# An expert's rank from the sign of a score difference, in two fused operations, in a one-core transformer block

## The chip, the core and the metric

The kernel runs on one core of a Trainium2 chip. The metric is the device time of one execution in microseconds (us). The engines are named as in the profile: PE (TensorE, matrix products), PEld (its weight loads), DVE (VectorE), ACT (ScalarE), POOL (GpSimd) and SP (SyncE, which here mostly issues DMAs). Every engine takes its own instructions strictly in the order in which the program emits them; between engines, semaphores hold an instruction back until its data or its buffer is there.

## The reference

A block of two attention layers, each followed by a mixture-of-experts feed-forward layer, on 2048 tokens of 256 numbers. What matters here is how each token's two experts are chosen:

```
scores = jax.nn.sigmoid(x @ router_w.T)              # [tokens, 8 experts]
selection_scores = scores + expert_bias
_, top_idx = jax.lax.top_k(selection_scores, TOPK)   # TOPK = 2
top_scores = jnp.take_along_axis(scores, top_idx, axis=-1)
top_scores = top_scores / (top_scores.sum(-1, keepdims=True) + 1e-09)
```

`top_k` puts the lower index first where two scores are equal. Everything is float32. The feed-forward layer runs twice (kernel layers 1 and 3), with the same weights.

## The kernel before, in words

The tokens are cut into four blocks (`tb`) of 512. The program is emitted by one long loop of *steps* (from line 1255 on). A step emits, in this order: matrix products of attention scores for two pairs of heads (L508); the reads of their results, by DVE for row maxima (L540, L552) and by ACT for exponentials (L603, L605); then, twice, a *half*, in which waiting small pieces are emitted; and at the end of the step the *fill*: pieces of the shared feed-forward (PE L921, L934 and L948; ACT L924; DVE L925, L937 and L950) and of the routed experts (PE L993, L1009 and L1030; DVE L995, L1017 and L1019).

The small pieces of DVE wait in the queue `vector`. Each stands there with a cost in us that the planner assumes for it. In each half the loop adds to an allowance and emits pieces while the allowance is above zero:

```
share = BUSY.get(i, VECTOR)                                  # VECTOR = 0.8
spare = min(spare + busy * share, 2 * busy * share)
while vector and spare > 0:
    us, f = vector.popleft()
    f()
    spare -= us
```

Here `i` counts the steps and `busy` is 1 while attention steps remain, 4 after that, so the allowance is capped at 1.6 in most steps. What is emitted for PE, ACT, POOL and SP comes from other queues (`queue`, `fill`, `routed_fill`, `moves`, `later`), whose budgets don't read the allowance.

Routing runs once for each block in each of the two feed-forward layers: eight times. `routing` (L718) emits the router's products and, at the end of that step, a tanh on ACT (L752). Then its DVE pieces follow, each appended to `vector` when the one before has been emitted (`chain`, L257): `selection` (L756, L757: the score and the biased score `sel`), `better` (L761), `equal` (L764), `equal_before` (L767), `ranks` (L770, L771), `best` (L774 to L776), `chosen` (no instruction), then `shares` (L780 to L783). The rank of an expert is the number of experts with a larger score, and of those with an equal score and a lower index; `other` and `own` are two views of `sel`, so each of these operations has 4 x 8 x 8 = 256 numbers in each of 128 partitions. `lower` is a constant table of ones and zeros, one where the other expert's index is lower.

Where a routing completes a group of tokens (seven of the eight times), `chosen` also starts `places` (L801): `either` (L822), a count on PE (L829) that is emitted in the step after `either`, and again DVE pieces (`along`, `tiling`, `starts`, `pick`, `rows_known`, `passed`, `weights`, `pick`, L844 to L882). They give the rows to which POOL scatters the tokens (L898) and the experts whose weights it fetches (L971). The pieces of a layer norm (L284 to L314) go through the same queue `vector`: `stats`, `guess` (L292 to L294), `newton` (L299 to L301) and `apply`.

In the order of time the eight routings are those of layer 1, blocks 0 to 3, and of layer 3, blocks 0 to 3. They are called routing 1 to 8 below. In routings 4 and 6 the loop emits a projection of the attention (PE L697, DVE L705) from `queue` in the same two halves.

Of the kernel before, what the change touches and what calls it, by code (L numbers as in the profile page):

```python
# [16 lines left out]
ALU = mybir.AluOpType  # L17
# [34 lines left out]
def tile_block(ctx: ExitStack, tc: tile.TileContext, a: dict, out: bass.AP):  # L52
    nc = tc.nc
# [93 lines left out]
    lower = const.tile([P, NX, NX], F32, tag="lower", name="lower")  # L147
# [67 lines left out]
    def free_one(at):  # L215
        n, j = at[:2]
        returned.add((n, j))
        if (n, 1 - j) in returned:
            returned.difference_update([(n, 0), (n, 1)])
            pairs.append(n)  # L220
# [16 lines left out]
    def alone(at, ins):  # L237
        n, j, user, other = at
        own = ins.ins.engine
        tc.add_to_no_dep_group(f"user{user}_{own}", ins.ins)  # L240
        for e in (mybir.EngineType.PE, mybir.EngineType.DVE, mybir.EngineType.Activation):
            if e != own and other is not None:
                tc.declare_no_dep(ins.ins, group=f"user{other}_{e}", reason="another bank of the pair")
# [13 lines left out]
    def chain(*steps):  # L257
        def add(i):
            if i < len(steps):
                q, f, *us = steps[i]  # L260
                f = partial(run, i, f)
                if us:
                    q.append((us[0], f))
                elif i:
                    after(0, partial(q.append, f))
                else:
                    q.append(f)

        def run(i, f):
            f()  # L270
            add(i + 1)

        add(0)
# [54 lines left out]
    def few_outputs(kind, xt, weights, to):  # L328
        bank, pr = one(kind)
        for c in range(EC):  # L330
            for t in range(TB // P):
                alone(bank, nc.tensor.matmul(
                    pr[t * FEW : (t + 1) * FEW, 0:P],
                    weights[:, c, :],
                    xt[:, c, t * P : (t + 1) * P],
                    start=(c == 0),
                    stop=(c == EC - 1),
                ))
        alone(bank, nc.scalar.copy(to, pr[:, 0:P]))
        free_one(bank)  # L340

    def tokens_down(kind, rows):
        bank, pt = one(kind)
        pt = pt[:, 0:P]
        alone(bank, nc.tensor.transpose(pt, rows, ident))
        return bank, pt.rearrange("p (t e) -> p t e", e=FEW)
# [364 lines left out]
    def sorting(ln, tb):  # L711
        return next(f for f, (l, tbs) in enumerate(SORTED) if l == ln and tb in tbs)
# [5 lines left out]
    def routing(ln, tb, then):  # L718
        xt = xts[ln, tb]
        nt = TB // P  # L720
        n = f"{ln}_{tb}"
        f = sorting(ln, tb)
        tbs = SORTED[f][1]
        t0 = tbs.index(tb) * nt
        if t0 == 0:
            picks[f] = (
                fp.tile([P, 2, len(tbs) * nt, NX], F32, tag="picked", name=f"picked{f}", bufs=1),
                fp.tile([P, len(tbs) * nt, NX], F32, tag="cw", name=f"cw{f}", bufs=1),
            )
        m0, m1 = (picks[f][0][:, k, t0 : t0 + nt, :] for k in range(2))  # L730
        cw = picks[f][1][:, t0 : t0 + nt, :]

        def small(x, shape):
            return fp.tile(shape, F32, tag=x, name=f"{x}{n}", bufs=1)

        sg, sel, rank, top = (small(x, [P, nt, NX]) for x in ("sg", "sel", "rank", "top"))
        tot = small("tot", [P, nt])
        full = [P, nt, NX, NX]
        gt, eq = small("gt", full), small("eq", full)
        other = sel.unsqueeze(2).broadcast_to(full)  # L740
        own = sel.unsqueeze(3).broadcast_to(full)

        rated = small("rated", [P, P])

        def scores():
            few_outputs("router", xt, late["router"], rated)
            chain(*after_scores)


        def rates():  # L750
            bank, pt = tokens_down("rated", rated)
            alone(bank, nc.scalar.activation(sg, pt[:, :, 0:NX], AF.Tanh, scale=0.5))  # L752
            free_one(bank)

        def selection():
            nc.vector.tensor_scalar(sg, sg, 0.5, 0.5, ALU.mult, ALU.add)  # L756
            nc.vector.tensor_tensor(sel, sg, late["ebias"].unsqueeze(1).broadcast_to([P, nt, NX]), ALU.add)  # L757


        def better():  # L760
            nc.vector.tensor_tensor(gt, other, own, ALU.is_gt)  # L761

        def equal():
            nc.vector.tensor_tensor(eq, other, own, ALU.is_equal)  # L764

        def equal_before():
            nc.vector.tensor_tensor(eq, eq, lower.unsqueeze(1).broadcast_to(full), ALU.mult)  # L767

        def ranks():
            nc.vector.tensor_tensor(gt, gt, eq, ALU.add)  # L770
            nc.vector.tensor_reduce(rank, gt, AX.X, ALU.add)  # L771

        def best():
            nc.vector.tensor_scalar(m0, rank, 0.5, None, ALU.is_lt)  # L774
            nc.vector.tensor_scalar(m1, rank, 1.0, None, ALU.is_equal)
            nc.vector.scalar_tensor_tensor(top, rank, 1.5, sg, ALU.is_lt, ALU.mult)  # L776


        def shares():
            nc.vector.tensor_reduce(tot, top, AX.X, ALU.add)  # L780
            nc.vector.tensor_scalar(tot, tot, 1e-9, None, ALU.add)
            nc.vector.reciprocal(tot, tot)
            nc.vector.scalar_tensor_tensor(  # L783
                cw, top, 0.5, tot.unsqueeze(2).broadcast_to([P, nt, NX]), ALU.mult, ALU.mult
            )

        def chosen():
            then()
            vector.append((0.7, shares))

        v = [(selection, 0.35), (better, 0.45), (equal, 0.45), (equal_before, 0.45), (ranks, 0.9), (best, 0.55)]
        queue.append(scores)
        after_scores = ((closing, rates), *[(vector, x, us) for x, us in v], (vector, chosen, 0.0))

# [325 lines left out]
    def ffn(ln, tb):  # L1120
        f = sorting(ln, tb)
        last = tb == SORTED[f][1][-1]
        routing(ln, tb, partial(places, f) if last else lambda: None)
        h0, y0 = shared_pieces(ln, tb, 0)
        h1, y1 = shared_pieces(ln, tb, 4)
        y1.append((0.0, partial(shared_end, ln, tb)))
        fill.extend(h0 + h1[:2] + y0 + h1[2:] + y1)
        if last:
            sorting_now.add(f)
# [293 lines left out]
```

## Time and profile before

| what | value |
|---|---|
| time of three runs | median 1227.33 us, from 1226.06 to 1230.43 |
| the profiled execution's own time | 1226.37 us |
| its span, from first to last instruction | 1224.7 us |
| mean granted TensorE clock | 0.978 |
| instructions in all | 21600 |
| ACT busy | 473.8 us (39%) |
| POOL busy | 385.2 us (31%) |
| first operation of the rank (L761) in routings 1, 2, 3, 4 | at 176.00, 317.63, 471.54 and 598.27 us |
| and in routings 5, 6, 7, 8 | at 747.08, 895.14, 974.32 and 1129.35 us |

The durations come from one profiled execution. A row of the groups reads: line, engine, operation, result and source, shapes, count, then busy us and mean ns of one, then the idle time of the engine before such instructions with what ended it. A row of the timeline reads: start, duration, engine, line, operation, and in brackets the idle time before it and who ended that. An instruction's duration is longer than the distance to the start of the next one where the two overlap, so a saving is read from the distances of starts, not from durations.

### The profile page before, as it was taken

What the parts mean: (1) busy time and instruction counts of PE and PEld (TensorE: products, weight loads), DVE (VectorE), ACT (ScalarE), POOL (GpSimd) and SP (SyncE); (2) the same over time, 40 slices, a digit from 0 to 9 for tenths busy, and PEclk for the clock granted to TensorE, in tenths of its full rate; (3) what the DMA queues carried; (4) which work ended last, traced back from release to release, by engine and by line L of the source; (5) the groups of instructions that cost most, each with busy time, mean ns of one, the idle gap of its engine ahead of it and who ended that gap; (6) DMA issues with size and microseconds to landing.
All of it is one profiled execution on the core that took longest, in us unless ns stands there. A gap on an engine that the chain in (4) does not pass through costs nothing.

```text
span 1224.7 us, 21600 instructions
## 1 busy us (share of the span) xinstructions
PE 1151.4 (94%) x7684; PEld 661.8 (54%) x7684; DVE 803.8 (66%) x2308; ACT 473.8 (39%) x838; POOL 385.2 (31%) x568
## 2 busy tenths in 40 slices
PE   5889999999999999998999999999999999998985
PEld 2343444465655556465654656456654553666563
DVE  5677878658776868646776867565678675335444
ACT  1356544435443542443234444444313445331110
POOL 3131201523252311543242212345311135142643
PEclk8789999999999999999999999999999999998998
DMA  7131010313442433434541423245422113464763
GB/s 232 42 123 33 11 43 25 126 50 114 147 148 70 133 111 97 135 105 123 172 151 56 139 78 99 78 134 173 126 70 70 56 43 111 149 202 139 250 231 108
DMA packets 87500, 137.85 MB, mean 113 GB/s; under 512 B 24016, under 2 KB 58704, under 8 KB 87264
## 3 DMA queue, kind: packets, MB, share of 16 engines
q1 hardware_dynamic: 68064, 66.63, 17.8%
q0 software_dynamic: 17520, 68.74, 17.5%
q8 instruction: 61, 1.00, 0.3%
q10 hardware_dynamic: 1808, 1.10, 0.3%
q14 instruction: 47, 0.39, 0.1%
HBM read 93.80 MB, written 31.59 MB: 102 GB/s over the span
## 4 chain that ended last, share of the span: by engine, by line
PE 44%; issue 4%; DVE 4%; DMA 3%; ACT 1%; SPq 1%; POOL 1%; POOLq 0%; ACTq 0%; DVEq 0%
PE ps L508 10%; PE ps L921 6%; PE ps L948 6%; PE ps L934 5%; PE ps L634 5%; PE ps L1009 4%; PE ps L1030 2%; PE ps L396 2%; DMA xr<-sx 1%; PE ps L697 1%; PE ps L993 1%; DMA wt<-in_w_e_dram,wrow 1%; PE ps L357 1%; PE ps L468 1%; ACT e L603 1%
## 5 line engine op out<-in xcount | busy, mean ns | idle before, releaser
L540 DVE CUSTOM_DVE_ANT_0 junk<-ps,hidden 128x384 f32<-128x384 f32 (+3 forms) x512 | 250.4, 489 | 86.2 <-PE ps L508 60.1
L508 PE MATMUL ps<-k,q 32*128 32x512 f32 (+3 forms) x1536 | 286.3, 523 | 18.0 <-DVE nm L540 6.4
L508 PE MATMUL ps<-q,k 32*128 32x512 f32 (+3 forms) x1536 | 279.9, 517 | 3.9 <-DVE nm L540 2.2
L603 ACT ACTIVATE e<-ps 128x512 f32<-128x512 f32 (+1 forms) x320 | 160.1, 552 | 221.9 <-PE ps L508 211.4
L614 POOL TENSOR_SCALAR_AFFINE_SELECT e<-e 128x256 f32<-128x256 f32 x256 | 100.9, 409 | 369.0 <-ACT e L603 240.5
L508 PEld LDWEIGHTS ps<-k,q 32*128 32x128 f32 x1536 | 111.1, 189 | 129.3 <-issue 45.6
L552 DVE TENSOR_REDUCE mx<-ps 128x2 f32<-128x1024 f32 x128 | 150.7, 1217 | 26.0 <-PE ps L508 25.2
L605 ACT ACTIVATE e<-ps 128x1024 f32<-128x1024 f32 (+1 forms) x160 | 151.1, 944 | 23.1 <-PE ps L508 14.5
L634 PE MATMUL ps<-e,v 128*17 128x512 f32 (+3 forms) x1536 | 137.1, 493 | 5.7 <-POOL e L614 3.8
L971 POOL DMA_INDIRECT wt<-in_w_e_dram,wrow x98 | 94.4, 963 | 131.8 <-PE ps L1030 111.2
L508 PEld LDWEIGHTS ps<-q,k 32*128 32x128 f32 x1536 | 114.0, 184 | 38.4 <-issue 7.7
L921 PE MATMUL ps<-xt,w 128*128 128x512 f32 x256 | 124.5, 609 | 0.5
L934 PE MATMUL ps<-xt,w 128*128 128x512 f32 x256 | 123.3, 604 | 0.0
L948 PE MATMUL ps<-w,h 128*128 128x256 f32 x512 | 117.1, 382 | 0.0
L948 PEld LDWEIGHTS ps<-w,h 128*128 128x128 f32 x512 | 95.3, 190 | 22.6 <-ACT e L603 5.1
L1009 PE MATMUL ps<-xst,wt 128*128 128x128 f32 x784 | 98.1, 278 | 1.0 <-DMA wt<-in_w_e_dram,wrow 1.0
L1009 PEld LDWEIGHTS ps<-xst,wt 128*128 128x128 f32 x784 | 93.4, 194 | 2.0 <-DMA wt<-in_w_e_dram,wrow 1.5
L634 PEld LDWEIGHTS ps<-e,v 128*17 128x17 f32 x1536 | 41.9, 98 | 97.2 <-issue 60.7
L898 POOL DMA_INDIRECT sx<-xh,pos x64 | 62.5, 976 | 80.3 <-PE ps L634 25.8
L925 DVE SCALAR_TENSOR_TENSOR h<-h,ps 128x512 f32<-128x512 f32 x64 | 43.8, 685 | 63.7 <-ACT h L924 63.5
L1044 POOL DMA_INDIRECT yg<-sy,pos x64 | 62.3, 974 | 68.7 <-DVE x L1052 37.4
L934 PEld LDWEIGHTS ps<-xt,w 128*128 128x128 f32 x256 | 46.0, 190 | 57.7 <-issue 43.9
(142 smaller groups left out, 1166.8 us busy)
## 6 DMA issues: line engine op xcount, KB each, us to landing
w<-in_w_dram SPq DMA_DIRECT2D x64, 256.0 KB
xr<-sx SPq DMA_DIRECT2D x53, 256.0 KB
sy<-yt SPq DMA_DIRECT2D x53, 256.0 KB
sx<-hidden POOLq DMA_DIRECT2D x2, 2944.0 KB, 15.6
q<-stage SPq DMA_DIRECT2D x24, 224.0 KB
uc<-u SPq DMA_DIRECT2D x128, 32.0 KB
rb<-dr SPq DMA_DIRECT2D x128, 32.0 KB
den<-u SPq DMA_DIRECT2D x128, 2.0 KB
```

What stands on the lines that cost most here:

```text
L508: nc.tensor.matmul(pair[:, j, at : at + c1 - c0], lhs[r, l0 : l0 + P], rhs[r, c0:c1], start=True, stop=True)
L540: r = nc.vector.tensor_tensor_reduce(junk[:, 0:wd], pair[:, j, at : at + wd], hidden_keys[:, TB - wd : TB], -1.0, -NEG, ALU.add, ALU.min, ...
L552: nc.vector.tensor_reduce(mx[:, 2 * pr : 2 * pr + 2, ts[0]], pair, AX.X, ALU.max, negate=True)
L603: alone(at, nc.scalar.activation(e[:, 2 * pr + j, c0:TB], pair[:, j, c0:TB], AF.Exp))
L605: nc.scalar.activation(e[:, 2 * pr : 2 * pr + 2, c0:TB], pair[:, :, c0:TB], AF.Exp)
L614: nc.gpsimd.affine_select(out=blk, in_=blk, compare_op=ALU.is_ge, fill=0.0, base=0, pattern=[[0, 2], [1, P]], channel_multiplier=-1,)
L634: alone(bank, nc.tensor.matmul(av[g * 32 : g * 32 + D + 1, c0:TB], v[:, i, 0 if multi_query(w) else g4 * 4 + g, :], e[:, g, at : at + TB - ...
L921: mm = nc.tensor.matmul(pg, loaded[i][:, k, 0:P], xts[ln, tb][:, k, :], start=(k == 0), stop=(k == EC - 1))
L934: mm = nc.tensor.matmul(pl, w[:, k, P : 2 * P], xts[ln, tb][:, k, :], start=(k == 0), stop=(k == EC - 1))
L948: alone(bank, nc.tensor.matmul(po[:, k, :], hs[i0 + i][:, cols], late["w3"][:, c0 + i, :], start=(i == 0), stop=(i == 3)))
L971: nc.gpsimd.indirect_dma_start(w, None, a["w_e"], by_row(wrow[:, j : j + 1]))
L1009: mm = nc.tensor.matmul(gu[:, j, k, :], w[:, cols], xt[:, c, k, :], start=(c == 0), stop=(c == EC - 1))
```

## The change

The comparison and the test for equality no longer read the two views of `sel` each. One operation takes their difference; two fused operations compare it with zero, one multiplying by the table `lower`, the other adding the first one's result. The piece `equal` is gone from the list, with its planned 0.45 us; the other planned costs stand as they were.

```diff
-        def better():
-            nc.vector.tensor_tensor(gt, other, own, ALU.is_gt)
-
-        def equal():
-            nc.vector.tensor_tensor(eq, other, own, ALU.is_equal)
+        def ahead():
+            nc.vector.tensor_tensor(gt, other, own, ALU.subtract)
 
         def equal_before():
-            nc.vector.tensor_tensor(eq, eq, lower.unsqueeze(1).broadcast_to(full), ALU.mult)
+            nc.vector.scalar_tensor_tensor(
+                eq, gt, 0.0, lower.unsqueeze(1).broadcast_to(full), ALU.is_equal, ALU.mult
+            )
 
         def ranks():
-            nc.vector.tensor_tensor(gt, gt, eq, ALU.add)
+            nc.vector.scalar_tensor_tensor(gt, gt, 0.0, eq, ALU.is_gt, ALU.add)
             nc.vector.tensor_reduce(rank, gt, AX.X, ALU.add)
...
-        v = [(selection, 0.35), (better, 0.45), (equal, 0.45), (equal_before, 0.45), (ranks, 0.9), (best, 0.55)]
+        v = [(selection, 0.35), (ahead, 0.45), (equal_before, 0.45), (ranks, 0.9), (best, 0.55)]
```

## The prediction, made before the run

> **What bounds the kernel now.** I read the page's busy times and its chain that ended last, then PE's own waits.
>
> ```profile
> PE 1151.4 (94%) x7684; PEld 661.8 (54%) x7684; DVE 803.8 (66%) x2308; ACT 473.8 (39%) x838; POOL 385.2 (31%) x568
> ...
> PE 44%; issue 4%; DVE 4%; DMA 3%; ACT 1%; SPq 1%; POOL 1%; POOLq 0%; ACTq 0%; DVEq 0%
> ```
>
> PE is busy for 94% of the span, so 73 us of idle PE are all that a faster DVE could win anywhere. DVE has a third of its time free. The change touches DVE alone, eight times, so the question at each place is whether PE stands still there for DVE's sake. Of PE's waits, two belong to lines that follow a routing:
>
> ```profile
> PE ps L508 <- DVE nm L540: 8.6, 10, 2.7
> ...
> PE ps L508 <- DVE h L925: 1.7, 3, 0.8
> ```
>
> The columns are us in total, times, and the longest.
>
> **What an operation costs.** From the groups by shape:
>
> ```profile
> L1052 DVE SCALAR_TENSOR_TENSOR x<-yg,share,x 128x256 f32<-128x256 f32 x64 | 30.7, 483 | 6.7 <-DMA yg<-sy,pos 5.6
> ...
> L1017 DVE SCALAR_TENSOR_TENSOR ht<-ht,ps 128x256 f32<-128x256 f32 x53 | 22.2, 419 | 58.3 <-ACT ht L1014 58.3
> ...
> L767 DVE TENSOR_TENSOR eq<-eq,lower 128x256 f32<-128x256 f32 x8 | 3.4, 430 | 0.3
> L761 DVE TENSOR_TENSOR gt<-sel 128x256 f32<-128x256 f32 x8 | 3.4, 424 | 0.3
> L770 DVE TENSOR_TENSOR gt<-gt,eq 128x256 f32<-128x256 f32 x8 | 3.4, 423 | 0.2
> ...
> L764 DVE TENSOR_TENSOR eq<-sel 128x256 f32<-128x256 f32 x8 | 3.3, 418 | 0.0
> ```
>
> The removed operation (L764) lasts 418 ns, but the distance of starts is what counts. Routing 1 in the timeline:
>
> ```profile
> 176.00 0.42 DVE L761 TENSOR_TENSOR gt<-sel 128x256 f32<-128x256 f32 x1
> 176.34 0.42 DVE L764 TENSOR_TENSOR eq<-sel 128x256 f32<-128x256 f32 x1
> 176.79 0.42 DVE L767 TENSOR_TENSOR eq<-eq,lower 128x256 f32<-128x256 f32 x1
> 177.25 0.43 DVE L770 TENSOR_TENSOR gt<-gt,eq 128x256 f32<-128x256 f32 x1
> 177.71 0.42 DVE L771 TENSOR_REDUCE rank<-gt 128x32 f32<-128x256 f32 x1
> 178.04 0.68 DVE L925 SCALAR_TENSOR_TENSOR h<-h,ps 128x512 f32<-128x512 f32 x1
> ...
> 178.77 1.13 PE L508 MATMUL ps<-q,k 32*128 32x512 f32 x4 [0.79 <-DVE h L925]
> ```
>
> An operation that needs the result just ahead of it starts 0.45 or 0.46 us after that one; L764 needs nothing from L761 and starts 0.34 us after it. In the changed code every operation of the rank needs the one before. So a rank falls from 0.34 + 0.45 + 0.46 + 0.46 = 1.71 us (start of L761 to start of L771) to 0.45 + 0.46 + 0.46 = 1.37 us: 0.34 us saved, not 0.42. Eight times that is **2.7 us of DVE**.
>
> The two fused operations with both sources in SBUF are not in the trace in this form. The nearest rows: L1017, with one source in PSUM, takes 419 ns; L1052, both in SBUF but with a scalar from memory, 483 ns. Plain two-source rows take 423 to 430. I take the price of L767 and L770 (no change) and keep +0.06 us for each (483 against 423). A far upper bound is the fused row of twice the size, L937, at 685 ns: +0.26 us each. Below the plain row there is no room to gain but 0.01 us (419).
>
> [...]
>
> **What moves.** Here the planner's arithmetic decides. A routing begins with the allowance at its cap, 1.6. Before: `selection` 1.25, `better` 0.80, `equal` 0.35, `equal_before` -0.10, end of the half; next half +0.8 = 0.70: `ranks` -0.20; next step 0.60: `best` 0.05, `chosen`, `either` -0.15; then 0.65: `shares`. After: `selection` 1.25, `ahead` 0.80, `equal_before` 0.35, `ranks` -0.55; next half 0.25: `best` -0.30; next step 0.50: `chosen`, `either` 0.30, `shares` -0.40. So `best` comes a step earlier, ahead of that step's fill; `either` and hence the count on PE stay in the same step. While the count is awaited the allowance returns to its cap, and the two versions run level, except for 0.05. Walking on, I find `rows_known` and `weights`, which feed POOL, in the same steps as before in all seven groups. So the orders of PE, ACT, POOL and SP stay as they are; only DVE's changes.
>
> In the first step the move of `best` eats the saving. Before, from the start of L761 to that of the fill behind L771: 2.04 to 2.07 us. After: 1.37, then 0.45 (L774 needs the rank; routing 8 shows that distance, 1131.07 to 1131.52), then 0.30 for the three small operations (1131.52 to 1131.82) = 2.12 us, some **0.07 us later**. The step after that has the 0.30 us less.
>
> Place by place:
> - Routing 1: PE stood idle 0.79 us for L925, the instruction right behind. L925 comes 0.07 us later: **+0.07 us** on the path (up to +0.19 with both fused operations at 483 ns). The 0.3 us won in the next step end in DVE's own idle 3.76 us before the L540 at 186.48.
> - Routing 2: behind the fill DVE idles 0.27 us for ACT at L1017. In the next step PE waits 0.50 us for L925 (326.57), but that L925 itself waited 0.26 us for ACT: nothing either way.
> - Routings 3, 5 and 7: PE is busy for 16.46 of 16.50, 16.00 of 16.00 and 15.59 of 15.70 us from the rank on: 0.
> - Routings 4 and 6: `ranks` now precede the first L705, which comes 0.57 us later (1.37 + 0.34 against 1.14); the second hardly moves. PE shows no wait for either; in routing 6 the load for L921 at 898.64 follows L1017's end by 0.1 us, so 0 to +0.13.
> - Routing 8: DVE idles 0.90 us for ACT (L1017 at 1133.98) before its chain to the end starts. That cover swallows the 0.34. If it were gone, 0.34 us would come off the end.
>
> The 0.05 left over matters once more. After routing 1 a layer norm's pieces follow at once, and with 0.05 more the allowance is still a rounding remainder above zero after the fourth `stats`; so `guess` (three instructions, 0.60 us from 206.91 to 207.51) is emitted a step earlier, between these:
>
> ```profile
> 202.42 0.18 DVE L285 BATCH_NORM_AGGREGATE mv<-st 128x2 f32<-128x6 f32 x1
> 202.52 0.67 DVE L937 SCALAR_TENSOR_TENSOR h<-h,ps 128x512 f32<-128x512 f32 x1
> 203.11 0.68 DVE L647 TENSOR_TENSOR u<-u,ps 128x512 f32<-128x512 f32 x1
> ...
> 203.84 0.70 PE L508 MATMUL ps<-q,k 32*128 32x512 f32 x2
> ```
>
> L647 ends at 203.79 and PE's next products start at 203.84: they need that bank. With `guess` ahead L647 ends 0.6 us later; PE has other products until about 204.0, so I put the loss at **+0.4 us** (0 to 0.6). Behind routing 4 one `pick` (0.51 us) moves ahead of an L937 in the same way, beside 3.69 us of PE work that doesn't wait: 0.
>
> **Sum.** +0.07 + 0.4 + about 0 = **+0.5 us** on the profiled 1226.37 (its span 1224.7 and 1.67 around it): 1226.9. The median stands 0.96 above that execution, so I predict **1227.8 us**. A measurement of this kernel tells about 0.3% (3.7 us) from no change; this is far inside.
>
> **Rivals.**
> - *The saving reaches the end.* If every place were on PE's path, 8 x 0.34 = 2.7 us: 1224.6. For it: PE waits for L540 and L925 8.6 and 1.7 us in all. Against: none of the eight places shows such a wait that the saving reaches. Still inside 0.3%. Chance 0.10.
> - *Slower: the fused operations run at half speed.* At 685 ns each the fill behind a rank comes 0.07 + 0.52 = 0.59 us later, and with all eight places exposed 4.7 us, with `guess` 5.1: 1232.4. It decides from about 0.46 us exposed per routing (3.7 over eight). For it: nothing but the far row. Against: L1052, and PE's cover in five places. Chance 0.06, of which 0.04 beyond 0.3%.
> - *The shift stirs DMA timing.* DVE's order changes when POOL's gathers and SP's loads are released, and three executions of one program already spread from 1226.06 to 1230.43, 0.36%. Either sign, 1223 to 1231.5; it is decided by whether a transfer that PE waits for (L993 for its rows, 5.9 us in all) starts later. Chance 0.12: 0.05 beyond 0.3% faster, 0.07 slower.
> - *It doesn't do what it says*: a difference that rounds to zero would only send a token elsewhere; the tile counts are fixed, so the time would be the forecast's.
>
> The forecast itself has 0.72. **Chances**: same 0.72 + 0.10 + 0.02 = 0.84, faster 0.05, slower 0.07 + 0.04 = 0.11. The range takes the first rival's end below, 1224.6, and the 0.3% bound above, 1231.0, short of the half-speed end.
>
> **What would show it.** Two fused rows near 425 to 485 ns, x8 each; starts from the difference to the reduction 1.37 to 1.5 us apart; L774 ahead of the fill in the rank's step; PE's wait for L925 near 178.8 at 0.8 to 1.0 us; a new PE wait for L647 near 204. Orders of PE and POOL unchanged. I am wrong if the fused rows are near 690 ns, or if PE's work shifts by whole steps.

## The result and the profile after

| | before | after |
|---|---|---|
| median of 13 runs each | 1225.87 us | 1232.36 us |
| lowest to highest | 1220.60 to 1231.17 | 1227.41 to 1234.33 |
| profiled execution, span | 1226.37, 1224.7 us | 1232.89, 1231.2 us |
| mean granted TensorE clock of it | 0.978 | 0.974 |

The ratio of after to before is 1.0047, with a 95% interval from 1.0029 to 1.0065. The changed kernel is **slower by about 0.5%** (some 6 us), and its median lies above the predicted range. Its 13 times stand in two clumps, five from 1227.4 to 1229.5 us (mean granted clock 0.978 or 0.979) and eight from 1231.8 to 1234.3 (0.974 to 0.976); the profiled execution belongs to the upper one.

In the page of after, the busy times and the chain that ended last:

```profile
PE 1155.0 (94%) x7684; PEld 663.4 (54%) x7684; DVE 802.2 (65%) x2300; ACT 473.4 (38%) x838; POOL 384.3 (31%) x568
...
PE 43%; DMA 5%; DVE 4%; SPq 2%; issue 2%; ACT 1%; POOL 0%; POOLq 0%; ACTq 0%; DVEq 0%
```

DVE has the eight operations less (2300 for 2308), but only 1.6 us less busy time where 2.7 us were forecast (eight times 0.34; the removed operation overlapped its neighbours). PE has the same 7684 products and is busy 3.6 us *longer* with them. So two things are to be found: what lengthened DVE's other work, and what slowed PE's products.

The groups of DVE by shape, after (busy us, then mean ns of one):

```profile
L764 DVE SCALAR_TENSOR_TENSOR eq<-gt,lower 128x256 f32<-128x256 f32 x8 | 3.4, 425 | 0.3
L769 DVE SCALAR_TENSOR_TENSOR gt<-gt,eq 128x256 f32<-128x256 f32 x8 | 3.4, 424 | 0.3
...
L774 DVE TENSOR_SCALAR picked<-rank 128x32 f32<-128x32 f32 x8 | 2.5, 311 | 0.0
```

The two fused operations take 425 and 424 ns, as the plain ones did. The odd row is the third: the second small operation of `best`, on 32 numbers, now averages 311 ns. Before, it was one line lower and took 201:

```profile
L775 DVE TENSOR_SCALAR picked<-rank 128x32 f32<-128x32 f32 x8 | 1.6, 201 | 0.0
```

Eight times that difference is 0.9 us, and the timeline of routing 1 shows it in one instance:

```profile
178.38 0.42 DVE L770 TENSOR_REDUCE rank<-gt 128x32 f32<-128x256 f32 x1
178.83 0.18 DVE L773 TENSOR_SCALAR picked<-rank 128x32 f32<-128x32 f32 x1
178.88 1.26 POOL L684 TENSOR_TENSOR uc<-uc,rb 128x512 f32<-128x512 f32 x1 [20.65 <-DMA rb<-dr]
178.92 1.25 DVE L774 TENSOR_SCALAR picked<-rank 128x32 f32<-128x32 f32 x1
180.09 0.18 DVE L775 SCALAR_TENSOR_TENSOR top<-rank,sg 128x32 f32<-128x32 f32 x1
180.19 0.68 DVE L924 SCALAR_TENSOR_TENSOR h<-h,ps 128x512 f32<-128x512 f32 x1
...
180.93 1.63 PE L508 MATMUL ps<-q,k 32*128 32x512 f32 x4 [1.94 <-DVE h L924]
```

POOL's multiplication of an attention result by its row factors (L684, two sources in SBUF) starts at 178.88; the DVE operation that starts 0.04 us later ends only when POOL does. Behind it stands L924, for which PE waits: 1.94 us, where it was 0.79. The same POOL operation ran in before, at the same place in the program, and nobody was held: the rank's reduction, L925 and L552 were DVE's work at that time, and they took 0.42, 0.68 and 1.2 us each as elsewhere. Line by line, the timeline of before holds it, and also, elsewhere, a DVE operation that it did hold:

```profile
177.83 1.27 POOL L684 TENSOR_TENSOR uc<-uc,rb 128x512 f32<-128x512 f32 x1 [20.60 <-DMA rb<-dr]
178.04 0.68 DVE L925 SCALAR_TENSOR_TENSOR h<-h,ps 128x512 f32<-128x512 f32 x1
...
332.62 1.74 DVE L844 TENSOR_TENSOR counts<-counts 128x32 f32<-128x32 f32 x3
333.05 1.27 POOL L684 TENSOR_TENSOR uc<-uc,rb 128x512 f32<-128x512 f32 x1 [4.93 <-issue]
```

Three L844 lasted 1.74 us together; the third of them alone took 1.29 us (its median is 0.19), until POOL's end at 334.32. Two more operations are held like this in after (L301 at 857.71, 1.23 us, and L1051 at 418.47, 1.45 us) and one more in before (L314 at 854.26, 1.27 us); with these, DVE's busy times add up.

The second question is answered by the table of stretches, of before and then of after. The columns are the stretch, its us, the busy us of PE, PEld, DVE, ACT and POOL, then the granted clock, the DMA share and GB/s:

```profile
181.00:184.00 3.00, 3.00 (x26) 0.70 (x28) 1.61 (x9) 0.00 (x0) 0.00 (x0) 1.00 0.28 87
```

```profile
181.00:184.00 3.00, 3.00 (x6) 1.06 (x7) 2.87 (x7) 1.02 (x1) 0.00 (x0) 0.57 0.02 5
184.00:187.00 3.00, 3.00 (x19) 0.82 (x21) 0.69 (x1) 0.00 (x0) 0.00 (x0) 0.86 0.14 16
```

After the longer wait PE was granted half its clock for 3.41 us (from 181.42 on). It is "busy" throughout. The counts of products in the two rows can't be compared, since other, smaller products fill this stretch in before; the same four products can, L934 in before and L933 in after:

```profile
179.83 1.98 PE L934 MATMUL ps<-xt,w 128*128 128x512 f32 x4
```

```profile
182.49 3.13 PE L933 MATMUL ps<-xt,w 128*128 128x512 f32 x4
```

That is the added busy time of PE.

Matching PE's products of the two traces one by one, after is 1.01 us later than before when it reaches routing 1 (the programs are the same until there), 2.15 us behind the wait, and 3.80 us from 182.5 on: 1.14 us by the wait and 1.65 us by the halved clock, **2.8 us from routing 1**. Another 1.3 us arises near 202, where the clock is halved again, and 3.3 us between 880 and 888: there PE waits 3.0 us for a load of `q` instead of 1.4 us for L1019, and the clock is halved once more. Some is given back elsewhere, and the end comes 6.5 us later than before's.

### The profile page after: what moved, and what is told of

Same layout as the page of the kernel before. It is cut to its first block, busy times and chain, and to the rows that moved or that the text cites. A ratio compares the mean times of both kernels' runs of the same rounds, so it can differ in the third digit from the quotient of the medians.

```text
span 1231.2 us, 21591 instructions
## 1 busy us (share of the span) xinstructions
PE 1155.0 (94%) x7684; PEld 663.4 (54%) x7684; DVE 802.2 (65%) x2300; ACT 473.4 (38%) x838; POOL 384.3 (31%) x568
## 4 chain that ended last, share of the span: by engine, by line
PE 43%; DMA 5%; DVE 4%; SPq 2%; issue 2%; ACT 1%; POOL 0%; POOLq 0%; ACTq 0%; DVEq 0%
PE ps L508 10%; PE ps L920 6%; PE ps L933 5%; PE ps L947 5%; PE ps L634 5%; PE ps L1008 4%; PE ps L1029 2%; DMA xr<-sx 2%; PE ps L697 1%; PE ps L396 1%; DMA dr<-den 1%; PE ps L992 1%; DMA q<-stage 1%; ACT e L603 1%; SPq L668 1%
## 5 line engine op out<-in xcount | busy, mean ns | idle before, releaser
L508 PE MATMUL ps<-k,q 32*128 32x512 f32 (+3 forms) x1536 | 286.3, 524 | 19.7 <-DVE nm L540 6.3
L508 PE MATMUL ps<-q,k 32*128 32x512 f32 (+3 forms) x1536 | 280.8, 519 | 5.0 <-DVE nm L540 2.2
L508 PEld LDWEIGHTS ps<-k,q 32*128 32x128 f32 x1536 | 110.8, 189 | 130.2 <-issue 50.6
L552 DVE TENSOR_REDUCE mx<-ps 128x2 f32<-128x1024 f32 x128 | 150.7, 1217 | 28.1 <-PE ps L508 27.4
L508 PEld LDWEIGHTS ps<-q,k 32*128 32x128 f32 x1536 | 114.2, 185 | 39.9 <-issue 7.4
L920 PE MATMUL ps<-xt,w 128*128 128x512 f32 x256 | 125.5, 613 | 0.5
L933 PE MATMUL ps<-xt,w 128*128 128x512 f32 x256 | 125.7, 614 | 0.0
L924 DVE SCALAR_TENSOR_TENSOR h<-h,ps 128x512 f32<-128x512 f32 x64 | 43.8, 685 | 66.2 <-ACT h L923 65.9
L933 PEld LDWEIGHTS ps<-xt,w 128*128 128x128 f32 x256 | 47.0, 194 | 59.4 <-issue 46.0
```

The costliest lines, as they stand in the source:

```text
L508: nc.tensor.matmul(pair[:, j, at : at + c1 - c0], lhs[r, l0 : l0 + P], rhs[r, c0:c1], start=True, stop=True)
L552: nc.vector.tensor_reduce(mx[:, 2 * pr : 2 * pr + 2, ts[0]], pair, AX.X, ALU.max, negate=True)
L920: mm = nc.tensor.matmul(pg, loaded[i][:, k, 0:P], xts[ln, tb][:, k, :], start=(k == 0), stop=(k == EC - 1))
L933: mm = nc.tensor.matmul(pl, w[:, k, P : 2 * P], xts[ln, tb][:, k, :], start=(k == 0), stop=(k == EC - 1))
```

## The experiments

The first four kernels ran on another chip, on which the kernel before takes 1263.78 us (median of 29 runs); the others on chips on which it takes 1226.06 (29 runs) and 1225.15 us (15). Each ratio is to the kernel before on the same chip. The theory after the result was: not the fused operations cost time, but the **order**. The planner's list is 0.45 us cheaper, so `best` comes ahead of L925, and in routing 1 it meets POOL. Rival B: the fused operations themselves. Rival G: the earlier `guess` and what follows it. A theory C, in the first two expectations, is that the change only redraws the timing of the DMAs by chance.

**The rank changed, the order kept** (the planned cost of the missing piece put on `ahead`):

```diff
-        v = [(selection, 0.35), (ahead, 0.45), ...
+        v = [(selection, 0.35), (ahead, 0.9), ...
```

> The changed kernel's four operations, but the difference is planned at 0.9 us, so that the allowance runs as before and DVE's order is that of the kernel before, less one operation per routing. Theory A (the moved pieces are to blame: in routing 1 the three operations of `best` stand ahead of L924 and beside a POOL multiplication, PE then idles 1.9 us and its clock is halved for 3.4 us; the operations themselves are harmless): ratio to the kernel before 0.997 to 1.001, PE's wait near 178 us back to about 0.5 to 0.8 us, no halved clock near 181. Theory B (the fused, dependent operations cost the time, wherever they stand): 1.003 to 1.006. Theory C (the change merely redraws the DMA timing by chance): 0.998 to 1.005, with long waits at other places.

Ratio 0.9999 (0.9975 to 1.0022). The timeline at routing 1:

```profile
177.68 0.68 DVE L924 SCALAR_TENSOR_TENSOR h<-h,ps 128x512 f32<-128x512 f32 x1
177.77 1.26 POOL L684 TENSOR_TENSOR uc<-uc,rb 128x512 f32<-128x512 f32 x1 [20.58 <-DMA rb<-dr]
...
178.41 1.13 PE L508 MATMUL ps<-q,k 32*128 32x512 f32 x4 [0.46 <-DVE h L924]
```

L924, with one source in PSUM, runs its usual 0.68 us beside POOL. PE's wait is 0.46 us: the 0.34 us saved by the rank arrive there (0.79 before), and even so the time does not move. The saving alone gives no gain that can be measured, and no cost of the fused operations shows.

**The order moved, the rank as before** (the kernel before, with `equal` planned at nothing):

```diff
-        v = [..., (equal, 0.45), (equal_before, 0.45), ...
+        v = [..., (equal, 0.0), (equal_before, 0.45), ...
```

> The kernel before with its five operations, but the test for equality planned at 0 us, so that the allowance, and with it the place of `best` and of the pieces behind it, is that of the changed kernel. Theory A: slow like the changed kernel, ratio 1.003 to 1.007 (DVE is 0.34 us later still at each place), with a long POOL-side stall of `best` in routing 1 and a halved clock near 181 us. Theory B: 0.998 to 1.001, since no fused operation is there. Theory C: no forecast but 0.998 to 1.005.

Ratio 1.0063 (1.0038 to 1.0089). L774 took 0.95 us beside POOL, PE waited 1.96 us, and the clock was halved for 6.83 us. A kernel without any fused operation is slow in the same way, so rival B falls.

**Routing 1 alone.** Two kernels with the changed rank. In the first, routing 1 keeps the order of before and the other seven are moved; in the second it is the other way round:

```diff
-        v = [(selection, 0.35), (ahead, 0.45), ...
+        v = [(selection, 0.35), (ahead, 0.9 if (ln, tb) == (1, 0) else 0.45), ...
```

```diff
-        v = [(selection, 0.35), (ahead, 0.45), ...
+        v = [(selection, 0.35), (ahead, 0.45 if (ln, tb) == (1, 0) else 0.9), ...
```

> The changed kernel, with the old order restored in routing 1 alone (difference planned at 0.9 us there); routings 2 to 8 as changed. Theory A: the loss of routing 1 and of its aftermath near 200 us is gone, ratio 0.998 to 1.002. Theory B: 1.003 to 1.006 less one eighth. If the loss sits in the other routings: 1.002 to 1.005.

> The counterpart: the changed order in routing 1 alone, the old order (difference planned at 0.9 us) in routings 2 to 8. Theory A: nearly the whole loss, ratio 1.002 to 1.006, with the halved clock near 181 us and, by its aftermath, near 202. Theory B: 1.003 to 1.006 too, but then e1 and e3 are slow as well. If the loss sits in the other routings: 0.998 to 1.001.

Ratios 0.9999 (0.9979 to 1.0019) and 1.0032 (1.0012 to 1.0052). Seven moved routings cost nothing that can be measured; one costs 0.3%. This speaks against theory C too: all the kernels so far that move routing 1 are slow (1.0047, 1.0063, 1.0032), and the two that keep it are not. The timeline of routing 1 moved alone:

```profile
178.25 1.26 POOL L684 TENSOR_TENSOR uc<-uc,rb 128x512 f32<-128x512 f32 x1 [20.58 <-DMA rb<-dr]
178.27 1.28 DVE L773 TENSOR_SCALAR picked<-rank 128x32 f32<-128x32 f32 x1
...
180.39 2.07 PE L508 MATMUL ps<-q,k 32*128 32x512 f32 x4 [1.96 <-DVE h L924]
```

Here POOL starts 0.02 us ahead of the first of the three small operations, and that one is held instead of the second. The clock was halved for 6.83 us behind it. The halved clock near 202 that I had expected as an aftermath isn't in this trace.

**`guess` put back where it was** (the 0.05 us that is left over goes to `starts` behind routings 1 and 4):

```diff
-        v = [(along, 0.65), (tiling, 0.7), (starts, 0.65), ...
+        v = [(along, 0.65), (tiling, 0.7), (starts, 0.7 if f in (0, 3) else 0.65), ...
```

> The changed kernel, but in the first and fourth group `starts` is planned at 0.70 instead of 0.65 us, which takes the 0.05 us of spare allowance away: the layer norm's `guess` near 204 us, the `passed` behind it and one `pick` near 614 us return to their old places, while `best` stays ahead of the fill in every routing. Theory A (the loss is `best` beside POOL's multiplication in routing 1, and the halved clock behind it): as slow as the changed kernel, ratio 1.002 to 1.006, wait of PE near 181 us again 1.9 us. Rival G (my forecast's own term: `guess` ahead of L936 and L647 costs PE some 0.4 us or, with a halved clock, more): 0.999 to 1.002.

Ratio 1.0030 (1.0011 to 1.0048). It is still slow, with a wait of 1.97 us and 6.83 us at half clock at routing 1, so rival G falls as the main cause. In the trace of after itself no product of PE waits for the moved `guess`: L292 to L294 run from 206.44 on, L647 at 208.44, and the L508 at 208.25 is not held by it.

**POOL's multiplication in four pieces**, so that DVE should be held for a quarter of the time:

```diff
-        nc.gpsimd.tensor_tensor(uc, uc, rb, ALU.mult)
+        for c in range(0, TB, P):
+            nc.gpsimd.tensor_tensor(uc[:, c : c + P], uc[:, c : c + P], rb[:, c : c + P], ALU.mult)
```

> The changed kernel, but POOL does each multiplication of L684 (128x512, 1.27 us) as four of 128x128. Theory A: the stalled operation of `best` waits for one quarter at most, 0.3 to 0.6 us instead of 1.25, PE's wait in routing 1 falls from 1.9 to some 1.0 to 1.3 us, the clock near 181 us isn't halved; ratio 0.999 to 1.003. If DVE is held by something other than a POOL operation in progress: L774 again 1.25 us, ratio 1.003 to 1.006.

Ratio 1.0022 (1.0003 to 1.0040). This expectation was half met. In the timeline (all line numbers one higher):

```profile
177.37 1.72 POOL L685 TENSOR_TENSOR uc<-uc,rb 128x128 f32<-128x128 f32 x4 [20.58 <-DMA rb<-dr]
177.40 0.47 DVE L774 TENSOR_SCALAR picked<-rank 128x32 f32<-128x32 f32 x1
...
178.96 1.68 PE L508 MATMUL ps<-q,k 32*128 32x512 f32 x4 [1.41 <-DVE h L925]
```

The held operation takes 0.47 us instead of 1.28: DVE is held for one piece, so it is indeed POOL's instruction that holds it. The twelve traces together say the same. Of the tensor-scalar, tensor-tensor and scalar-tensor-tensor operations with all their sources in SBUF, 25 started while an L684 (or a piece of it) had more time left than they usually take, and each of the 25 ended after it. In the same position stood 48 DVE operations that are reductions or have a source in PSUM, and none of them took over 1% longer than usual. But another one is held by a later piece (L776, 0.44 us), PE still waits 1.41 us, and the clock was halved all the same, for 6.83 us. What I had not counted on is that 1.41 us are enough for that.

**The delay by itself.** The kernel before, with sums that nothing reads put behind the rank in routing 1, ahead of L925. The sum was not held by POOL (it took 0.68 us from 178.78 on, with POOL's L684 running from 178.54 to 179.81), so this is a delay without the meeting. Two of them, and then one:

```diff
             nc.vector.tensor_reduce(rank, gt, AX.X, ALU.add)
+            if (ln, tb) == (1, 0):
+                for _ in range(2):
+                    nc.vector.tensor_reduce(small("delay", [P, 1]), hidden_keys, AX.X, ALU.add)
```

> The kernel before with two sums over a constant of 512 numbers (about 0.6 us of DVE each, nothing reads them) behind the rank in routing 1 alone, in front of L925; nothing else moves. Theory A with the clock as the second half of the loss: PE's wait there rises from 0.8 or 0.5 to 1.7 to 2.0 us, and a halved clock of 3.4 us follows at once, so PE's work behind routing 1 comes 2.7 to 3 us later though only 1.2 us were added. If the clock is independent of this wait: 1.2 us later, no halved clock.

> The kernel before with one such sum (about 0.6 us of DVE) behind the rank in routing 1; nothing else moves. If PE's clock follows PE's idle time in windows of 3.4 us, and 1.41 us of it were enough with POOL's multiplication in four: PE's wait 1.3 to 1.5 us and a halved clock right behind it, PE's work 2.5 to 3.5 us later than in the kernel before at the same place. If the clock needs a wait near 2 us: 0.6 us later, no halved clock.

One execution each, so they are read from their traces, not from their times (1229.37 and 1227.69 us). PE's lateness against before's trace, product by product, across routing 1:

| kernel | PE's wait | by the wait | half clock | by the clock | together |
|---|---|---|---|---|---|
| before | 0.79 us | | none | | |
| one sum | 1.39 | 0.59 us | 3.41 us | 1.65 us | 2.2 us |
| POOL in four | 1.41 | 0.62 | 6.83 | 3.29 | 3.9 |
| after | 1.94 | 1.14 | 3.41 | 1.65 | 2.8 |
| `guess` put back | 1.97 | 1.17 | 6.83 | 3.29 | 4.5 |
| two sums | 2.11 | 1.31 | 6.83 | 3.14 | 4.5 |

With one sum, the product behind the wait (L925 is L928 here) and the stretch after it:

```profile
180.11 1.13 PE L508 MATMUL ps<-q,k 32*128 32x512 f32 x4 [1.39 <-DVE h L928]
```

```profile
181.00:184.00 3.00, 3.00 (x6) 1.17 (x4) 2.35 (x10) 1.02 (x1) 0.00 (x0) 0.52 0.02 5
```

0.6 us of delay on DVE, without any help from POOL, became 2.2 us on PE, a little less than I had expected; the two sums cost 4.5 us, more than the 2.7 to 3 expected, since the halved clock lasted 6.83 us. Six traces are not in the table. In two of them (the order moved; routing 1 alone moved) PE waits 1.96 us here and the clock is halved; in the other four, with the order kept or the rank later, PE waits 0.46 us or not at all and the clock stays full behind it. So in the twelve traces the clock was halved behind each of the seven waits of 1.39 us or more at this place, and in none of the five with 0.79 us or less: the halved clock follows from the wait, and it costs more than what the wait grew by (1.65 to 3.29 us for 0.59 to 1.31).

**The rank later.** If the place is the cause, a routing whose rank stays behind L924 should lose PE's wait altogether. The planned costs are spread so that `ranks` falls into the next step, in all routings, and then in routing 1 alone with the order of before in the others:

```diff
-        v = [..., (ahead, 0.45), (equal_before, 0.45), (ranks, 0.9), (best, 0.55)]
+        v = [..., (ahead, 0.45), (equal_before, 1.65), (ranks, 0.45), (best, 0.25)]
```

```diff
-        v = [..., (ahead, 0.45), (equal_before, 0.45), (ranks, 0.9), (best, 0.55)]
+        if (ln, tb) == (1, 0):
+            v = [..., (ahead, 0.45), (equal_before, 1.65), (ranks, 0.45), (best, 0.25)]
+        else:
+            v = [..., (ahead, 0.9), (equal_before, 0.45), (ranks, 0.9), (best, 0.55)]
```

> A version meant to beat both: the four operations, with planned costs 0.35, 0.45, 1.65, 0.45 and 0.25 us (same sum as before), so that `ranks` and `best` both come a step later, behind that step's fill, and everything from `either` on stays where the kernel before has it. Theory A: PE's wait for L924 in routing 1 (0.46 to 0.79 us) goes, the 0.9 us of `ranks` now stands in the next step; ratio 0.997 to 1.001. Where `ranks` or `best` run beside POOL's multiplication they may stall up to 1.2 us; if that happens in front of an eviction that PE waits for, 1.001 to 1.005.

> The later rank (planned costs 0.35, 0.45, 1.65, 0.45, 0.25) in routing 1 alone, the old order in the others. If the gain of the version with all eight later (0.9985) comes from PE's wait in routing 1: ratio 0.997 to 1.000, no wait of PE for L924 near 177 us. If it comes from the other routings or from chance: 0.999 to 1.001.

Ratios 0.9985 (0.9965 to 1.0005), not distinct from no change, and 0.9964 (0.9943 to 0.9985), just below the expected 0.997. The second is the fastest version, faster than both kernels, at 1221.16 us where before takes 1225.15. Its routing 1 (L924 is L927 here, three lines being added; L769 is the second fused operation):

```profile
172.95 0.68 DVE L927 SCALAR_TENSOR_TENSOR h<-h,ps 128x512 f32<-128x512 f32 x1
...
173.68 1.13 PE L508 MATMUL ps<-q,k 32*128 32x512 f32 x4
173.95 1.26 POOL L684 TENSOR_TENSOR uc<-uc,rb 128x512 f32<-128x512 f32 x1 [20.57 <-DMA rb<-dr]
...
175.81 0.41 DVE L769 SCALAR_TENSOR_TENSOR gt<-gt,eq 128x256 f32<-128x256 f32 x1
```

PE no longer waits there, and POOL is done before the rank goes on. That the whole 0.36% is due to this is not shown: product by product, PE gains 1.24 us across this place, of the 4. (In its trace the clock is not halved once between 80 and 1000 us, where before's has one such stretch, at 576; 3.8 us of its lead arise ahead of routing 1, where the two programs are the same, most of it from 51 to 57 us, where before's clock was halved and its own was not.)

## Why the prediction was wrong, step by step

- **PE bounds the kernel, and the saved DVE time is hidden.** Right. With the order kept the ratio is 0.9999, although the 0.34 us per routing are there in the trace.
- **The fused operations cost what plain ones do.** Right: 425 and 424 ns, and the starts from the difference to the reduction lie 1.38 us apart where 1.37 were worked out. The slower rival put them at half speed, 685 ns, which no run shows. The slow result has another cause, as the kernel without fused operations shows.
- **What moves.** Right: comparing the order of the two traces, DVE's pieces moved as the walk through the allowance had them, and the orders of PE, ACT and SP are the same.
- **Routing 1: "+0.07 us on the path (up to +0.19)".** This is the step that failed. The place was right, since PE's wait for L925 near 178.8 is where the time is lost, but it was priced at 0.30 us for the three small operations, a duration from a routing in which POOL did not run beside them. In fact one of them took 1.25 us, and the wait grew by 1.14 us instead of 0.07. I had asked what the moved piece displaces on DVE, and not what the other engines do at that moment. The trace of before had the answer in two lines: POOL's L684 at 177.83, 0.12 us behind the start of the rank's reduction, and L844 held by the same operation at 333.05. What the runs show is which operations were held, and for how long: 1.25 us against 0.17 for L774, 0.47 us for the one held with POOL's work in quarters, and no delay for the reductions and for L924 (0.68 us beside POOL with the order kept). Why some were held and others not, no run here shows.
- **A wait of PE costs its length.** This was assumed without being said, and it is the second half of the failure. 1.14 us of wait brought 1.65 us more by the halved clock, and twice that in other executions. The stretches at half clock lasted 3.41 or 6.83 us, behind waits of 1.39 to 2.11 us.
- **`guess`: "+0.4 us (0 to 0.6)".** Wrong, but small: it cost 0, since L647 was released only at 208.44 in any case.
- **The other places at 0.** Right within what can be measured: seven moved routings together gave 0.9999.
- **The rivals.** None had this mechanism. The slower one had the right sign and a wrong cause, and the one on DMA timing does not explain why the loss follows routing 1.

With both terms, routing 1 should have been priced at 1.14 us plus 1.65 to 3.3 us, 2.8 to 4.4 us or 0.23 to 0.36%. The kernel that isolates it (1.0032) and the one with `guess` put back (1.0030) agree. After's own 1.0047 is somewhat more; whether the rest (the halved clocks near 202 and 885, the late load of `q`) belongs to the change or to the scatter between executions **stays open**, since the intervals overlap (1.0029 to 1.0065 against 1.0011 to 1.0048). For scatter: the product that waits for `q` there does so in nine of the twelve traces, for 1.1 to 3.0 us, and a halved clock near 195 shows in two other kernels too (routing 1 kept, and the rank later in all routings), neither of which is slow. The second of them has all three in its trace (half clock near 196 and 878, 2.95 us for `q`), and that execution is the slowest of its twelve, 1232.10 us at a median of 1223.42. The 1.0063 of the order moved with five operations is more than routing 1 explains, and the cause of that rest is open as well.

## What to carry to other kernels

A planned cost in a list that emits instructions decides their order, so a change that only makes work cheaper can move a piece ahead of the result that PE waits for; find where each piece lands, and read off the timeline what POOL does at that very moment. A short DVE operation on SBUF (no reduction) that starts beside such a POOL multiplication is to be priced at POOL's remaining time, not at its own (1.25 us for 0.17 here). And where PE already waits 0.8 us, the next 0.6 us may cost more than three times its length through the clock (0.6 us became 2.2), so the piece belongs behind the result that PE needs.

## What was not expected of the hardware

- A DVE operation of 32 numbers per partition, with a single source in SBUF, was held for 1.1 us by a POOL multiplication of 512 (L774 in after: 1.25 us, where its usual is 0.17). With a start 0.05 us ahead of POOL it ran free (L773 at 178.83), 0.04 us behind it it was held.
- PE's clock went to one half behind 1.4 us of idle PE (1.39 with one sum, 1.41 with POOL in four). In each trace the starts of the stretches at half clock lie whole multiples of 3.41 us apart, as on a fixed grid (in after they start at 181.42, 201.90, 580.78 and 884.56 us, 6, 111 and 89 such steps apart). I counted PE's idle time in each 3.41 us of that grid, from 80 to 1200 us in all twelve traces, where the clock was full. With 1.83 us or more, half a clock followed in 40 of 40 cases; with 1.39 to 1.80 us, in 12 of 35; with less, but some, in 5 of 2636, one of them the 0.79 us near 198 in after.
- So a wait's place on the grid seems to matter, and not only its length: with two sums a wait of 2.17 us near 878 was cut by the grid, left 1.40 us in the first part and did not halve the clock, while 1.39 us in one part near 178 halved it with one sum. What decides between 1.39 and 1.80 us is not settled here, nor why it is halved for 3.41 us in one execution and for 6.83 in another.
